# A two-layer decoder on one core: the inverse roots of six normalisation sites move from a bit-pattern seed with three Newton steps to a power on GpSimd with one

## The chip, the cores and the metric

The kernel runs on one core of a Trainium2 chip. The core has five engines, each with its own instruction queue that it works through in order: PE (TensorE, matrix products, with its weight loads shown as PEld), DVE (VectorE), ACT (ScalarE), POOL (GpSimd) and SP (SyncE, which here only issues DMAs). They wait for each other through semaphores. The metric is the time of one execution on the device in microseconds. The median of three executions of the kernel before is 1645.03 us (1643.46 to 1653.15).

## The reference

The inputs are x of 4 batches x 512 tokens x 512 features and a context of the same shape. Two layers of three blocks each follow, and after every block the sum with the block's input is normalised:

```
x = layernorm(x + L0_attention(x))            # stage A
x = layernorm(x + L0_cross_attention(x, ctx)) # stage B
x = layernorm(x + L0_ffn(x))                  # stage C, 8-bit activations, ternary weights
x = layernorm(x + L1_attention(x))            # stage D
x = layernorm(x + L1_cross_attention(x, ctx)) # stage E
x = layernorm(x + L1_ffn(x))                  # stage F, 4-bit weights

def layernorm(x): return (x - mean(x)) / sqrt(var(x) + 1e-5)   # over the 512 features
# at the end of L1_ffn: y / sqrt(mean(y * y) + 1e-6)
```

What the change touches is the inverse square root in these: one number per token, so 512 numbers per batch and normalisation. They lie in a tile of 128 partitions x 4.

## The kernel before

A task is one stage of one batch: A0 to A3, B0 to B3 and so on to F3, in that order. The function `lanes` runs up to two tasks at a time, step by step in turn: when a task reports "next", the following one is started beside it. So the last steps of B3, with its normalisation, lie beside the beginning of C0, those of C0 beside C1, and those of F0 beside F1. Further generators (`BESIDE`) load and prepare the weights of a later stage beside an earlier one. Within a task the class `Pipe` puts off an operation by so many steps. What this gives is the order of the program; a planner of the language then sets the order in each engine's queue from the dependences and its own estimates of the durations, and it may move an instruction past others, DMAs on SP too. Only the names below matter for the change.

**Roots.** `ln_rsqrt` (L185) adds 1e-5 to the four variances of a batch, giving `ve`, and then forms 1/sqrt(ve). For the pairs in `LOG_SEED` (all of A, B, D and E except B3 and E3) it takes a seed from ACT, exp(-0.5 ln ve), and one Newton step. For all others, which are B3, E3, C0 to C3 and F0 to F3, it calls `rsqrt`: two integer instructions on DVE (L162, L163) make a seed from the bit pattern, and three Newton steps follow. A Newton step is three DVE instructions (L170, L171, L172). Stage F calls `rsqrt` a second time, for the root of its own mean square (tile `fm`, after L1117). That is 14 calls of `rsqrt` in all: ten on an `ln` tile and four on an `fm` tile.

**Around the roots.** `ln_stats` (L176, L177) gathers mean and variance of a 128x512 tile. After the root `finish` normalises four such tiles (L200, DVE) and stores them (L203, SP); the next stage loads them again from DRAM (L217). In F the root of `fm` scales the four accumulators `facc` into x (L1121), which frees their four PSUM banks.

**Stage F.** For each of 11 chunks of the inner width, TensorE forms gate and up in four groups each (L1104, into PSUM tiles `fg`); ACT (L1062, L1065) and DVE (L1068) scale the groups and add them up, and so free the banks; POOL adds a part (L1072); ACT applies Silu (L1076), DVE multiplies (L1080), ACT and POOL split the product into a high and a low part (L1085, L1086), and TensorE adds the second product into `facc` (L1095). There are eight PSUM banks, four of which `facc` holds.

**Stage C.** TensorE forms `pg` and `pu` (L645, L647), DVE and ACT make the gated product (L616, L617, L621, L623), POOL its low part (L624), TensorE the Hadamard transform, which goes through DRAM (`had_scratch`, stored at L636, loaded again as `z`). In the second half DVE takes maxima (L659) and quantises (L680), and TensorE forms `dn` (L699), which DVE adds (L703).

Of the kernel before, what the change touches and what calls it, by code (L numbers as in the profile page):

```python
# [14 lines left out]
I32 = mybir.dt.int32  # L15
U8 = mybir.dt.uint8
AF = mybir.ActivationFunctionType
ALU = mybir.AluOpType
# [4 lines left out]
P = 128  # L23
NT = 4
MAGIC = 12582912.0
RSQRT_SEED = float(0x5F3759DF)
O_BUFS, T_BUFS, X_BUFS, W_BUFS = 69, 13, 12, 4


# [12 lines left out]
class Pipe:  # L42


    def __init__(self):
        self.todo = []
# [21 lines left out]
class Net:  # L68
    def __init__(self, ctx, tc, args):
        self.tc = tc  # L70
        self.nc = tc.nc
        self.a = args
        self.n = 0
        pool = lambda name, **kw: ctx.enter_context(tc.tile_pool(name=name, **kw))
        self.const = pool("const", bufs=1)
        self.op = pool("op", bufs=O_BUFS)
        self.tp = pool("tp", bufs=T_BUFS)
        self.xp = pool("xp", bufs=X_BUFS)
        self.wp_ = pool("wp", bufs=W_BUFS)
        self.small = pool("small", bufs=4)  # L80
        self.psum = pool("psum", bufs=8, space=PSUM)
        nc = self.nc
        tc.keep_in_program_order(nc.scalar.preload_act_table_set(LOG_EXP))
        self.ident = self.c("ident", [P, P])
        make_identity(nc, self.ident)
        self.ident16 = self.c("ident16", [P, P], BF16)
        nc.vector.tensor_copy(self.ident16, self.ident)
        self.ones = self.c("ones", [P, P])
        nc.gpsimd.memset(self.ones, 1.0)
        scratch = lambda name, shape: nc.dram_tensor(name, shape, F32, kind="Internal").ap()  # L90
        self.had_scratch = scratch("had_scratch", (2, 2048, 512))
        self.xd = [args["x"]] + [scratch(f"x{i}", (B, S, D)) for i in range(1, 6)] + [args["out"]]
        self.bg, self.table = {}, None
        self.gu, self.dn = {}, []
        self.pre = {}
        self.w1 = {}
        self.mean, self.scale = {}, {}
        self.tern = {name: {} for name in self.TERNARY}
# [58 lines left out]

    def rsqrt(self, ve, s):

        nc = self.nc  # L160
        sh, y, t = s[:, 0:4], s[:, 4:8], s[:, 8:12]
        nc.vector.tensor_scalar(sh.bitcast(I32), ve.bitcast(I32), 1, None, ALU.logical_shift_right)  # L162
        nc.vector.tensor_scalar(y.bitcast(I32), sh.bitcast(I32), -1.0, RSQRT_SEED, ALU.mult, ALU.add)  # L163
        for _ in range(3):
            self.newton(ve, y, t)
        return y

    def newton(self, ve, y, t):
# [1082 lines left out]
```

## Time and profile before

| | |
|---|---|
| median of three executions | 1645.03 us (1643.46 to 1653.15) |
| profiled execution, own time | 1649.59 us |
| its span | 1647.9 us |
| mean granted TensorE clock | 0.982 |
| DVE: the two integer instructions of a seed, x14 each | some 0.16 us each, undisturbed |
| DVE: one instruction of a Newton step, 128x4, median | 0.154 to 0.161 us |
| stage F from F0's first normalisation to the end | from about 1315 us |

The profile is one execution. Its page gives the busy time of each engine, groups of instructions by source line, and the chain of waits: from the last instruction back to what released it, step by step. The line numbers are those of the kernel before. A timeline row gives start, duration, engine, line, operation, output and inputs, and, in brackets, how long the engine had stood idle before and what released it. Releasers are inferred.

### The profile page before, as it was taken

What the parts mean: (1) busy time and instruction counts of PE and PEld (TensorE: products, weight loads), DVE (VectorE), ACT (ScalarE), POOL (GpSimd) and SP (SyncE); (2) the same over time, 40 slices, a digit from 0 to 9 for tenths busy, and PEclk for the clock granted to TensorE, in tenths of its full rate; (3) what the DMA queues carried; (4) which work ended last, traced back from release to release, by engine and by line L of the source; (5) the groups of instructions that cost most, each with busy time, mean ns of one, the idle gap of its engine ahead of it and who ended that gap; (6) DMA issues with size and microseconds to landing.
All of it is one profiled execution on the core that took longest, in us unless ns stands there. A gap on an engine that the chain in (4) does not pass through costs nothing.

```text
span 1647.9 us, 25494 instructions
## 1 busy us (share of the span) xinstructions
PE 1543.2 (94%) x8215; PEld 1106.6 (67%) x8246; DVE 1244.6 (76%) x2684; ACT 1011.3 (61%) x2177; POOL 666.1 (40%) x672
## 2 busy tenths in 40 slices
PE   7999999999999899899999999999998989999995
PEld 5888785444545664467777767777676766686874
DVE  6486589999875678967575666756879899979795
ACT  5333337988777777777696755968543444454542
POOL 6663654556435204420434342342333344333332
PEclk9999999999999999999999999999999999999998
DMA  6043344454125524861433323233445432011000
GB/s 244 29 147 122 122 162 138 133 171 159 52 95 176 186 82 138 245 176 62 130 76 78 78 81 109 69 79 76 154 153 178 142 102 61 24 54 51 1 26 25
DMA packets 103237, 180.76 MB, mean 110 GB/s; under 512 B 16561, under 2 KB 18609, under 8 KB 103105
## 3 DMA queue, kind: packets, MB, share of 16 engines
q1 hardware_dynamic: 98976, 170.69, 33.2%
q0 software_dynamic: 4128, 8.46, 2.1%
q8 instruction: 65, 1.06, 0.3%
q14 instruction: 68, 0.55, 0.1%
HBM read 111.98 MB, written 41.94 MB: 93 GB/s over the span
## 4 chain that ended last, share of the span: by engine, by line
PE 59%; DVE 17%; ACT 9%; DMA 6%; issue 5%; POOL 3%; SPq 1%; DVEq 0%; ACTq 0%; POOLq 0%
PE fg L1104 7%; PE facc L1095 6%; PE dT L881 3%; PE bo L458 2%; ACT de L871 2%; DVE bsm L434 2%; DVE x L200 2%; PE pu L647 2%; PE bT L213 2%; DMA z<-had_scratch 2%; PE pg L645 2%; PE dn L699 2%; PE do L901 2%; PE dq L150 2%; PE bs L486 2%
## 5 line engine op out<-in xcount | busy, mean ns | idle before, releaser
L1068 DVE SCALAR_TENSOR_TENSOR fg<-fg,gs,fg 128x512 f32<-128x512 f32 x220 | 162.3, 744 | 36.5 <-PE fg L1104 17.3
L867 DVE CUSTOM_DVE_ANT_0 de<-ds,negm,thr 128x128 f32<-128x128 f32 (+3 forms) x256 | 126.3, 545 | 34.3 <-PE ds L856 31.2
L1104 PE MATMUL fg<-fxh,gu 128*128 128x512 f32 x352 | 144.2, 410 | 7.6 <-DVE fg L1068 4.6
L871 ACT ACTIVATE de<-de,dm 128x128 f32<-128x128 f32 (+3 forms) x256 | 143.1, 563 | 12.4 <-DVE dm L867 11.9
L1104 PE MATMUL fg<-fxl,gu 128*128 128x512 f32 x352 | 139.1, 395 | 0.0
L442 POOL TENSOR_SCALAR be<-be,bsm 128x512 f32<-128x512 f32 x128 | 95.8, 760 | 104.5 <-DVE bsm L440 74.8
L624 POOL TENSOR_TENSOR hl<-g,hh 128x512 fp32r<-128x512 f32 x64 | 84.1, 1321 | 114.1 <-ACT hh L623 93.4
L1072 POOL TENSOR_TENSOR fg<-fg,fg 128x512 f32<-128x512 f32 x44 | 60.8, 1382 | 128.6 <-ACT fg L1065 89.4
L436 ACT ACTIVATE be<-bs,bsm 128x512 f32<-128x512 f32 x128 | 87.2, 688 | 31.9 <-DVE bsm L434 30.0
L798 POOL TENSOR_TENSOR dql<-dqf,dqh 128x512 fp32r<-128x512 f32 x32 | 41.2, 1289 | 155.1 <-ACT dqh L797 120.9
L881 PE MATMUL dT<-ident,de 128*128 128x128 f32 x640 | 90.3, 279 | 7.6 <-ACT de L871 5.8
L1104 PEld LDWEIGHTS fg<-fxh,gu 128*128 128x128 f32 x352 | 67.1, 191 | 38.1 <-DVE fg L1068 14.2
L881 PEld LDWEIGHTS dT<-ident,de 128*128 128x128 f32 x640 | 72.3, 142 | 26.1 <-ACT de L871 12.7
L1062 ACT ACTIVATE fg<-fg,gs 128x512 f32<-128x512 f32 x88 | 60.4, 686 | 39.9 <-PE fg L1104 39.5
L713 PE MATMUL had<-had,z 128*128 128x128 f32 x512 | 74.0, 289 | 10.5 <-DMA z<-had_scratch 10.2
L434 DVE TENSOR_REDUCE bsm<-bs 128x1 f32<-128x512 f32 x128 | 83.3, 671 | 0.0
L1095 PE MATMUL facc<-p4h,fhh 128*128 128x512 f32 x176 | 71.7, 408 | 8.9 <-DVE fg L1068 6.2
L713 PEld LDWEIGHTS had<-had,z 128*128 128x128 f32 x512 | 66.9, 198 | 18.7 <-DMA z<-had_scratch 7.7
L458 PE MATMUL bo<-bpT,cT 128*64 128x512 f32 x256 | 76.8, 618 | 2.9 <-DVE bpT L449 1.6
L213 PEld LDWEIGHTS bT<-ident,be 128*128 128x128 f32 x512 | 55.0, 141 | 34.1 <-issue 12.3
L213 PE MATMUL bT<-ident,be 128*128 128x128 f32 x512 | 73.2, 281 | 3.8 <-POOL be L442 2.1
L1065 ACT ACTIVATE fg<-fg,gs 128x512 f32<-128x512 f32 x44 | 30.3, 688 | 75.1 <-PE fg L1104 75.1
(332 smaller groups left out, 4676.2 us busy)
## 6 DMA issues: line engine op xcount, KB each, us to landing
x<-x SPq DMA_DIRECT2D x176, 256.0 KB, 3.1
had_scratch<-hw SPq DMA_DIRECT2D x64, 256.0 KB, 2.0
z<-had_scratch SPq DMA_DIRECT2D x64, 256.0 KB, 6.1
stk<-dqh SPq DMA_DIRECT2D x192, 64.0 KB, 2.0
tw<-in_wg_t SPq DMA_DIRECT2D x32, 256.0 KB, 3.7
tw<-in_wu_t SPq DMA_DIRECT2D x32, 256.0 KB, 3.7
tw<-in_wd_t SPq DMA_DIRECT2D x32, 256.0 KB, 2.9
p<-in_gu_p SPq DMA_DIRECT2D x22, 256.0 KB, 2.8
```

The source lines that it names most:

```text
L213: self.nc.tensor.transpose(pt[:, i * P : (i + 1) * P], srcs[i][:, j * P : (j + 1) * P], self.ident)
L434: nc.vector.tensor_reduce(sm[:, h : h + 1], ps, AX.X, ALU.max, negate=True)
L436: nc.scalar.activation(e, ps, AF.Exp, bias=sm[:, h : h + 1], accum_out=sm[:, 2 + h : 3 + h])
L442: nc.gpsimd.tensor_scalar(es[h][i], es[h][i], sm[:, 4 + h : 5 + h], 1.0, ALU.mult, ALU.mult)
L458: nc.tensor.matmul(po[0][h * 64 : h * 64 + 64, :], cT[j][:, c : c + 64], pTs[h], start=j == 0, stop=j == NT - 1)
L713: nc.tensor.matmul(ps[:, c * P : (c + 1) * P], z[g * 4 + c][:, i * P : (i + 1) * P], self.had16, start=True, stop=True)
L867: nc.vector.tensor_tensor_reduce(es[i], ps, self.negm[:, 384 - P * i :], -1.0, self.thr[:, i : i + 1], ALU.add, ALU.min, n4[:, i : i + 1])
L871: nc.scalar.activation(es[i], es[i], AF.Exp, bias=n4[:, i : i + 1], scale=-1.0, accum_out=den[:, hh * 4 + i : hh * 4 + i + 1])
L881: nc.tensor.transpose(pt[:, o + (i - j) * P : o + (i - j + 1) * P], es[i][:, j * P : (j + 1) * P], self.ident)
L1068: nc.vector.scalar_tensor_tensor(y[u], ps, s, y[u], ALU.mult, ALU.add)
L1095: nc.tensor.matmul(acc[t], h[l][:, c], self.dn[i][r], start=i == 0 and n == 0, stop=i == 10 and n == 2)
L1104: nc.tensor.matmul(ps, self.gu[i, u][:, g * P : (g + 1) * P], xT[g][n], start=n == 0, stop=n == 1)
```

## The change

`rsqrt` no longer makes a seed from bits. GpSimd raises `ve` to the power of -1/2 by a `tensor_tensor` with a constant tile of -0.5 (`mhalf`, 128x4, set once at the start), and one Newton step on DVE follows instead of three. The 14 calls stay where they are in the program; those that take their seed from ACT are not touched. Each call so has one POOL instruction and three DVE instructions instead of eleven DVE instructions; in all DVE has 112 instructions fewer and POOL 15 more (14 powers and the memset).

```diff
-RSQRT_SEED = float(0x5F3759DF)
...
+        self.mhalf = self.c("mhalf", [P, NT])
+        nc.gpsimd.memset(self.mhalf, -0.5)
...
     def rsqrt(self, ve, s):
 
-        nc = self.nc
-        sh, y, t = s[:, 0:4], s[:, 4:8], s[:, 8:12]
-        nc.vector.tensor_scalar(sh.bitcast(I32), ve.bitcast(I32), 1, None, ALU.logical_shift_right)
-        nc.vector.tensor_scalar(y.bitcast(I32), sh.bitcast(I32), -1.0, RSQRT_SEED, ALU.mult, ALU.add)
-        for _ in range(3):
-            self.newton(ve, y, t)
+        y, t = s[:, 4:8], s[:, 8:12]
+        self.nc.gpsimd.tensor_tensor(y, ve, self.mhalf, ALU.pow)
+        self.newton(ve, y, t)
         return y
```

`newton`, which both call, is unchanged: t = y*y; t = -0.5*t*ve; y = (t + 1.5)*y.

The planner orders the queues anew. On DVE the Newton step that waits for the power follows L185 or L1117 directly at the four `fm` roots, in B3 and in C3, and elsewhere after one other instruction; the four normalisations (L200) come earlier against the neighbours. On POOL the power stands between neighbours whose order is almost the same as before. On SP, in C1 and C2, the stores of x and their reloads come ahead of the first stores to `had_scratch` and of one weight load. In the changed kernel the lines behind `rsqrt` are numbered two lower (L170 becomes L168, L1117 becomes L1115).

## The prediction, on record before the changed kernel had run

> **What bounds the kernel.** I read the engine totals first, then the gaps of TensorE, then the chain of waits around the code that changes.
>
> ```profile
> PE 1543.2 (94%) x8215; PEld 1106.6 (67%) x8246; DVE 1244.6 (76%) x2684; ACT 1011.3 (61%) x2177; POOL 666.1 (40%) x672
> ```
>
> TensorE computes for 94% of the span, so removed DVE time counts only where TensorE stands still for DVE, or after its last matmul. The fourteen roots lie at: the end of B3 (469.7 us), C0 (597 to 604), C1 (624 to 635), C2, C3 (within 700 to 790), E3 (1315 to 1326), two for each of F0, F1, F2 (from 1406.6, 1485.2 and 1562), and two for F3 in the tail. Here is the chain of waits that ended last, cut to 1405 to 1412 (some pieces between are not shown), where F0 ends and F1 begins (columns: start us, us, who):
>
> ```profile
> 1406.70 0.09 DVE fm L1117
> ...
> 1406.81 0.18 DVE fm L162
> ...
> 1407.02 1.19 DVE fm L163
> ...
> 1408.23 1.20 DVE fm L170
> ...
> 1409.45 0.04 DVE fm L171
> ...
> 1409.53 0.76 DVE fg L1068
> ...
> 1410.33 1.59 PE facc L1095 x4
> ```
>
> The reader is to see that TensorE waits here for L1068, which empties a PSUM bank, and L1068 stands in DVE's queue behind the root. Two of its tiny 128x4 instructions take 1.19 and 1.20 us instead of some 0.16. The timeline says why:
>
> ```profile
> 1406.87 1.30 POOL L1072 TENSOR_TENSOR fg<-fg,fg 128x512 f32<-128x512 f32 x1 [3.16 <-DVE fm L1117]
> ...
> 1408.11 1.28 POOL L1086 TENSOR_TENSOR fhl<-fg,fhh 128x512 fp32r<-128x512 f32 x1
> ...
> 1410.33 0.50 PE L1095 MATMUL facc<-p4h,fhh 128*128 128x512 f32 x1 [1.92 <-DVE fg L1068]
> ```
>
> L163 and L170 begin just after POOL's two 1.3 us instructions and end with them, while L1068 (one operand in PSUM) runs at 0.75 beside POOL elsewhere. I call that a collision. TensorE loses 1.92 us, and in the next 4.1 us its granted clock is 0.58 (1.7 us more). The same pair of collisions and the same 1.92 us gap stand at 1488.87 and 1567.39.
>
> In the tail (timeline from 1628) TensorE and POOL are done and DVE works alone:
>
> ```profile
> 1631.27 0.17 DVE L162 TENSOR_SCALAR fm<-fm 128x4 int32<-128x4 int32 x1
> ...
> 1632.86 0.16 DVE L170 TENSOR_TENSOR fm<-fm 128x4 f32<-128x4 f32 x1
> ...
> 1633.45 1.41 DVE L1121 SCALAR_TENSOR_TENSOR x<-facc,fm,x 128x512 f32<-128x512 f32 x2
> ```
>
> Eleven dependent instructions take 2.18 us, start to start 0.198 each; the last Newton step alone takes 1633.45 - 1632.86 = 0.59. The second root, 1639.78 to 1641.96, is the same again.
>
> **The price of a pow (p).** No row of before shows pow. The nearest rows on POOL (source line, out, shape, then busy us and mean ns):
>
> ```profile
> L581 POOL TENSOR_SCALAR cm<-cm 128x4 f32<-128x4 f32 x4 | 1.0, 251 | 1.6 <-DVE bsm L440 0.9 <-DVE am L669 0.4 <-DVE cm L578 0.3
> ...
> L142 POOL TENSOR_TENSOR wkl<-wk,wkh 128x512 fp32r<-128x512 f32 x1 | 1.7, 1729 | 0.0
> ```
>
> From below 0.25 us: same shape, plain arithmetic. From above 1.73, the longest plain instruction of POOL, as if each of four elements cost as much as 128 plain ones. I take 0.5: the 128x4 row is nearest, doubled because a power is a series and not one operation. A handover DVE to POOL is 0.09 (L1117 ends 1406.78, L1072 starts 1406.87), back 0.03 (L923 ends 1166.33, the L924 that waits for it starts 1166.36), together 0.12.
>
> First-use cost: the first tensor_tensor on POOL took 1.27 us, no more than the later 1.3, so no row shows code being loaded. [...]
>
> **Part by part.**
>
> *Tail, two roots.* Each loses 2.18 and gets 0.59 + 0.12 + 0.5 = 1.21. POOL's last work ended at 1626, so nothing collides. Gain 2 x 0.97 = 1.9 us, wholly on the path.
>
> *F0/F1, F1/F2, F2/F3, first root (fm).* In the new order L1117 is followed at once by the Newton step, which waits for pow. Behind it in DVE's queue stands the same L1068 that TensorE wants. On POOL pow lands between an L1086 and L1072 and finds POOL idle (since 1403.7). L1072's operands are there at 1406.74, so it starts right behind pow. So: pow 1406.87 to 1407.37; L1072 to 1408.7, L170 (two SBUF operands) stuck behind it; L1086 to 1410.0, L171 stuck; L172; L1068 at 1410.2 instead of 1409.53. That is 0.65 us more wait, three times: loss 2.0. If only L170 is caught, L1068 comes at 1409.0 (gain 0.5); if none, at 1408.0 (gain 1.5). I take two, as POOL is first at both. Then L1121 and the statistics, formerly behind six L1068, come right after the first; the four facc banks that they free stand in for those that the later L1068 free.
>
> *F0 to F2, second root (ln), and E3.* Its steps lie between L1068s: a lone 128x4 instruction there costs under 0.1 us, since the neighbours overlap it. So the eight removed save mainly collisions (L185 1.26, L163 1.18, L171 0.71, L172 0.67 in F0: 3.2 us). But TensorE has no gap from 1411 to 1440, so at F I credit nothing. pow is covered: one L1068 (0.7) lies between L185 and the waiting L170, against 0.12 + 0.5; cover ends at p = 0.6. POOL is idle at 1419.4 to 1424.9, where pow falls. The 1.00 gap at 1440.57, behind four norms (L200), moves forward with them. In E3 two collisions (L170 0.81, L171 1.27) stand before TensorE gaps of 0.67 and 0.44: gain 0.7.
>
> *C0 to C3 and B3.* In B3 and C3 no instruction lies between L185 and the wait. B3: L616 comes 0.5 us later, and one L621 falls behind all four norms (about 1.3). TensorE has no gap over 0.3 from 460 to 490, with four pg/pu pairs of work ahead: nothing. C0, C2, C3: no gap beside them that is put down to DVE: nothing. C1: 2.7 us of collisions, and a gap of 1.07 at 638.75 for L616 behind the norms: gain 0.5.
>
> *Moved transfers.* On SP in C1/C2 the stores and reloads of x3 now stand ahead of the first had_scratch stores and a w1 load; in F0 three packed-weight loads swap neighbours. The z reloads wait for the last stores, which keep their places: 0, with 1.5 either way. One added 128x4 memset, 0.09 us while POOL idles to 5.36: nothing.
>
> Sum: -1.9 + 2.0 - 0.7 - 0.5 = -1.1 us. Against the profiled execution's own 1649.6 that gives 1648.5; that execution was 4.6 above the median of the runs (1645.0), to which I apply the same difference: **1644**. One percent (16 us) is about what a measurement can tell from no change.
>
> **Rivals.**
> 1. *Pow is slow* (ends slower). In DVE's queue everything behind the waiting L170 stops. At most 14 sites pay per us of p: 2 in the tail, 3 fm, 4 ln in E and F above 0.6, 5 in B and C above 0.6. Net loss starts near p = 0.65. At 1.73: tail +0.5, fm 3 x 1.9, ln 4 x 1.1, B and C half of 5 x 1.2, less 1.2: +13, or 1658. Over 1% from p near 2; 5 us would give 1645 + 14 x 4.4 = 1707. For: nothing bounds a power. Against: only 512 elements.
> 2. *The collisions vanish at the F boundaries* (faster). L1068 comes 1.5 earlier, the gap shrinks to 0.4 and the low clock with it: 3 x (1.5 + 1.7) + 1.9 + 1.2 = 12.7, or 1632. For: gaps of 1.0 (1440.57) and 1.5 (1329.31) are followed by clock 1.00. Against: L1072 stands ready behind pow.
> 3. *It does not do what it says*: interleaved steps were free anyhow, and a pow of 0.8 to 1.4 eats the tail's gain (gone at 2.18 - 0.59 - 0.12 = 1.47) while the fm waits grow: at 1.4, tail -0.1, fm +4.7, ln +3.2, B and C +2, less 1.2, or +8.6: 1646 to 1654.
>
> **Numbers.** Forecast (p 0.25 to 0.8, 1641 to 1648): 0.55. Rival 3, 1646 to 1654: 0.2. Rival 2, part or whole: 0.13, a tenth of it over 1%. Rival 1, p over 1.4: 0.12, nearly all over 1%. The range 1636 to 1655 leaves out rival 1 and the far half of rival 2, under 0.2 together. Faster by over 1%: 0.02; within: 0.87; slower: 0.11.
>
> **What will show it.** A POOL row of fourteen 128x4 tensor_tensor at L162 of the new numbering, mean near 500 ns, none far longer. In the tail: from L1115 (old L1117) to the first L1119 some 1.4 us instead of 2.4. At the F boundaries: L168 and L169 at 1.2 us each and TensorE's gap at 2.0 to 2.6; if it is under 1 with clock 1.00, rival 2. I am wrong if pow takes over 1 us, or if TensorE waits for DVE in C.

## The result: 0.46% slower

The changed kernel takes 1655.59 us (median of 15 executions, 1649.66 to 1660.52); the kernel before, beside it on the same chip, 1647.28 us (15 executions). The ratio is 1.0046, with a 95% interval of 1.0034 to 1.0058: 7.6 us slower where 1.1 us faster was forecast, and 0.6 us beyond the end of the range given. The profiled execution of the changed kernel took 1654.74 us, its span is 1653.0 us; before it was 1649.59 and 1647.9. The forecast of 1644 stood on a median of three executions of the kernel before, 1645.0; with 15 it is 1647.3, so 2.3 us of the distance between 1644 and 1655.6 are the base and not the change. The prediction took 16 us for the least that can be told from no change; with 15 executions of each kernel the interval is 2 us to either side.

The engine totals of the changed kernel, from its page:

```profile
PE 1544.1 (93%) x8215; PEld 1107.9 (67%) x8246; DVE 1225.0 (74%) x2572; ACT 1011.8 (61%) x2177; POOL 676.0 (41%) x687
```

DVE has 112 instructions and 19.6 us of busy time less, and the kernel is slower all the same. The groups of POOL, split by shape (busy us and mean ns of one, then idle time before):

```profile
L162 POOL TENSOR_TENSOR ln<-ln,mhalf 128x4 f32<-128x4 f32 x10 | 10.3, 1029 | 48.5 <-DVE ln L183 31.3 <-PE pu L645 17.1
L162 POOL TENSOR_TENSOR fm<-fm,mhalf 128x4 f32<-128x4 f32 x4 | 4.1, 1017 | 14.7 <-DVE fm L1115 14.7
```

A power of 128x4 takes 1.02 to 1.03 us on average, where 0.5 was taken. The first one of the execution (469.77, at the end of B3) took 1.04.

The chain of waits at the boundary of F0 and F1, restricted to that stretch (start us, us, who):

```profile
1410.32 1.03 POOL fm L162
...
1411.37 1.24 DVE fm L168
...
1412.64 1.21 DVE fm L169
...
1413.96 0.76 DVE fg L1066
...
1414.76 1.19 PE facc L1093 x4
```

The timeline of the same place (start us, us, engine, line, operation; in brackets the idle time before, and what ended it):

```profile
1410.32 1.02 POOL L162 TENSOR_TENSOR fm<-fm,mhalf 128x4 f32<-128x4 f32 x1 [3.15 <-DVE fm L1115]
...
1411.31 1.27 POOL L1070 TENSOR_TENSOR fg<-fg,fg 128x512 f32<-128x512 f32 x1
1411.37 1.23 DVE L168 TENSOR_TENSOR fm<-fm 128x4 f32<-128x4 f32 x1 [1.13 <-POOL fm L162]
...
1412.54 1.27 POOL L1084 TENSOR_TENSOR fhl<-fg,fhh 128x512 fp32r<-128x512 f32 x1
...
1414.76 0.50 PE L1093 MATMUL facc<-p4h,fhh 128*128 128x512 f32 x1 [2.88 <-DVE fg L1066]
```

DVE now stands 1.13 us for the power, then runs into both collisions that the prediction expected, and TensorE's gap has grown from 1.92 to 2.88 us. The tail, from the timeline:

```profile
1637.20 0.17 DVE L1115 TENSOR_SCALAR fm<-fm 128x4 f32<-128x4 f32 x1 [7.14 <-ACT fsq L1112]
1637.45 1.02 POOL L162 TENSOR_TENSOR fm<-fm,mhalf 128x4 f32<-128x4 f32 x1 [5.36 <-DVE fm L1115]
1638.50 0.16 DVE L168 TENSOR_TENSOR fm<-fm 128x4 f32<-128x4 f32 x1 [1.13 <-POOL fm L162]
...
1639.09 1.41 DVE L1119 SCALAR_TENSOR_TENSOR x<-facc,fm,x 128x512 f32<-128x512 f32 x2
```

From L1115 to L1119 it is 1.89 us, before 2.38: each of the two roots gains 0.5. Elsewhere only E3 is seen to gain.

**Where the time went.** To compare two traces I take the start of each TensorE instruction, counted from the first one, and subtract: the offset. Its places are counted from there too and so are 6 us lower than in the timelines. Between the changed kernel and before it is about 0 up to 520 us, +2.1 at 580, +5.4 at 610 and +6.0 from 770 to 1200; it falls to +3.4 before the first boundary of F, gains some 0.9 at each of the three boundaries, and the tail takes 1.0 back. In these two executions the largest part thus arises in stages B3 to C3, for which the prediction had put down next to nothing.

### The profile page after: what moved, and what is told of

Its sections match the earlier page's. It is cut to its first block, busy times and chain, and to the rows that moved or that the text cites. A ratio compares the mean times of both kernels' runs of the same rounds, so it can differ in the third digit from the quotient of the medians.

```text
span 1653.0 us, 25402 instructions
## 1 busy us (share of the span) xinstructions
PE 1544.1 (93%) x8215; PEld 1107.9 (67%) x8246; DVE 1225.0 (74%) x2572; ACT 1011.8 (61%) x2177; POOL 676.0 (41%) x687
## 4 chain that ended last, share of the span: by engine, by line
PE 54%; DVE 19%; ACT 11%; DMA 6%; issue 5%; POOL 3%; SPq 1%; POOLq 0%; DVEq 0%; ACTq 0%
PE fg L1102 6%; PE facc L1093 5%; DVE bsm L432 3%; PE dT L879 3%; ACT de L869 2%; PE pu L645 2%; DVE x L198 2%; PE pg L643 2%; PE do L899 2%; DVE fg L1066 2%; PE dn L697 2%; PE dq L151 2%; PE dq L152 2%; PE dq L153 2%; PE bo L456 1%
## 5 line engine op out<-in xcount | busy, mean ns | idle before, releaser
L869 ACT ACTIVATE de<-de,dm 128x128 f32<-128x128 f32 (+3 forms) x256 | 143.2, 563 | 12.4 <-DVE dm L865 11.9
L1070 POOL TENSOR_TENSOR fg<-fg,fg 128x512 f32<-128x512 f32 x44 | 58.9, 1340 | 126.3 <-ACT fg L1063 78.6
L796 POOL TENSOR_TENSOR dql<-dqf,dqh 128x512 fp32r<-128x512 f32 x32 | 41.3, 1291 | 153.5 <-ACT dqh L795 121.1
L211 PEld LDWEIGHTS bT<-ident,be 128*128 128x128 f32 x512 | 54.9, 141 | 34.2 <-issue 10.4
```

What stands on the lines that cost most here:

```text
L211: self.nc.tensor.transpose(pt[:, i * P : (i + 1) * P], srcs[i][:, j * P : (j + 1) * P], self.ident)
L869: nc.scalar.activation(es[i], es[i], AF.Exp, bias=n4[:, i : i + 1], scale=-1.0, accum_out=den[:, hh * 4 + i : hh * 4 + i + 1])
```

## Experiments

Two theories at first. **Price**: DVE stands still for a power that takes 1.03 us, and TensorE follows. **Order**: the planner, which takes a power for a cheap instruction, moved the four norms ahead of the scales that the quantising in C waits for, and that costs. A third, **Collision**, puts the loss at the boundaries of F. Later, **Wait** (only the time in which DVE has nothing else in its queue costs) stands against **Neighbour** (a running power slows what runs beside it). Ratios are to the kernel before on the same chip, "us" is the ratio's difference times 1647; "stood" is DVE's time in standing for GpSimd's result at the roots, by the trace's list of waits.

| kernel | ratio (95% interval) | us | stood, us |
|---|---|---|---|
| changed kernel | 1.0046 (1.0034 to 1.0058) | +7.6 | 14.7 |
| the same again (11) | 1.0045 (1.0030 to 1.0060) | +7.4 | |
| 1 cheap instruction instead | 0.9993 (0.9982 to 1.0004) | -1.2 | 4.3 |
| 2 two powers in a row | 1.0120 (1.0102 to 1.0139) | +19.8 | 28.4 |
| 3 power in B3 and C alone | 1.0038 (1.0024 to 1.0052) | +6.3 | 4.0 |
| 4 power in E3 and F alone | 1.0023 (1.0012 to 1.0034) | +3.8 | 10.7 |
| 5 covered in B3 to C2 | 1.0028 (1.0014 to 1.0042) | +4.6 | 11.8 |
| 6 covered there and at fm | 0.9996 (0.9983 to 1.0009) | -0.7 | 10.4 |
| 7 no power, two steps | 1.0011 (0.9997 to 1.0026) | +1.8 | 0 |
| 8 before, fm root later | 0.9997 (0.9983 to 1.0011) | -0.5 | 0 |
| 9 two powers, covered | 1.0075 (1.0053 to 1.0097) | +12.4 | 19.1 |
| 10 power in E3 and F, fm covered | 0.9986 (0.9973 to 0.9999) | -2.3 | 9.2 |
| 12 cheap instruction in B3 and C alone | 1.0010 (0.9994 to 1.0026) | +1.6 | 0.6 |

### 1 and 2: the price alone, in the same order

```diff
-        self.nc.gpsimd.tensor_tensor(y, ve, self.mhalf, ALU.pow)
+        nc.gpsimd.tensor_scalar(y, ve, 0.0, 0.0005 if site[0] == "f" else 0.5, ALU.mult, ALU.add)
```

> All 14 powers are replaced by a cheap GpSimd instruction of the same place, tile and operand: y = 0*ve + a constant (0.5 on the ln tiles, 0.0005 on the fm tiles). Left out is the power itself, so the seed and with it the output is not the reference's. The order of the instructions on every engine is that of the changed kernel. The nearest row, L581, has 0.25 us for such an instruction, so the wait at each root should fall from 1.13 to some 0.35 us. Theory ORDER (the planner's new order in stage C, where the four norms stand ahead of the scales that the quantising waits for, carries the loss, +6 us by the end of C): the offset of TensorE against before stays at about +5 to +6 us at 800 to 1000 us; only the tail (2 x 0.78) and the three F boundaries (3 x 0.78) gain: some 1655.6 - 3.9 = 1651.7 us, still 4 us above before. Theory PRICE (the 1.03 us of a power, on which DVE stands, carries the loss): the offset at 800 us falls by up to 5 x 0.78 = 3.9 us as well, to about +2, and the time to 1648 us, equal to before. Theory COLLISION (the boundaries of F are what costs): two collisions stay at each boundary, with TensorE's gaps there at about 1.9 us again, and the stage from 1400 to 1640 us gives back its +2.8.

```diff
+        nc.gpsimd.tensor_tensor(sh, ve, self.mhalf, ALU.pow)
         nc.gpsimd.tensor_tensor(y, ve, self.mhalf, ALU.pow)
```

> Each root has two powers in a row on GpSimd, the first into a spare part of the tile: the price of a root rises from 1.03 to some 2.06 us; the order of all other instructions is that of the changed kernel. Theory PRICE: every site pays, up to 14 x 1.03 = 14 us above the changed kernel, 1665 to 1670 us. Theory ORDER: in C most of the wait lies beside other work; the tail pays 2.06, the three fm boundaries 3 x 1.03, a part of the rest: some +5 to +8, 1661 to 1664 us. Theory COLLISION: the fm boundaries alone pay, with TensorE's gap there 1 us longer each, and the tail: +5, 1661 us.

Measured: 1645.29 and 1667.31 us; Price had the second, and the first lies below what any of the three theories gave. The three kernels differ in nothing but what GpSimd needs for a root: 0.19, 1.02 and 2.03 us, and by the ratios the time moves by 8.7 and 12.2 us. Order falls as the main cause: with the same order the cheap instruction is no slower than before, and its offset at 800 us is +0.25. Collision falls too, as the larger part is in C. Against the time that DVE stands, the slope is 0.84 and 0.89 us per us: on average over the 14 roots nearly every microsecond of standing is paid. Root by root it is not the same.

The rows of the Newton steps that wait, in the changed kernel (timeline of DVE at the end of B3, in C0, C1, C2 and C3):

```profile
470.85 0.16 DVE L168 TENSOR_TENSOR ln<-ln 128x4 f32<-128x4 f32 x1 [1.16 <-POOL ln L162]
...
600.87 0.16 DVE L168 TENSOR_TENSOR ln<-ln 128x4 f32<-128x4 f32 x1 [0.56 <-POOL ln L162]
...
631.02 0.16 DVE L168 TENSOR_TENSOR ln<-ln 128x4 f32<-128x4 f32 x1 [0.57 <-POOL ln L162]
...
767.04 0.16 DVE L168 TENSOR_TENSOR ln<-ln 128x4 f32<-128x4 f32 x1 [0.56 <-POOL ln L162]
...
795.98 0.16 DVE L168 TENSOR_TENSOR ln<-ln 128x4 f32<-128x4 f32 x1 [1.16 <-POOL ln L162]
```

With the cheap instruction only the first and the last are left (experiment 1, same view):

```profile
470.56 0.16 DVE L177 TENSOR_TENSOR ln<-ln 128x4 f32<-128x4 f32 x1 [0.32 <-POOL ln L166]
...
789.30 0.16 DVE L177 TENSOR_TENSOR ln<-ln 128x4 f32<-128x4 f32 x1 [0.32 <-POOL ln L166]
```

As the order is the same, the offset between the three can be followed step by step, and each step has its place:

| root | DVE stands: exp. 1, changed, exp. 2 | step, exp. 1 to changed | step, changed to exp. 2 |
|---|---|---|---|
| B3 (470) | 0.32, 1.16, 2.15 | +1.0 (between 525 and 550) | +1.0 |
| C0 (600) | 0, 0.56, 1.55 | +0.66, and +1.7 behind it | +1.0 |
| C1 (630) | 0, 0.57, 1.55 | +0.65 | +1.0 |
| C2 (767) | 0, 0.56, 1.55 | +0.65 | +0.2 and +0.65, and +1.7 behind it |
| C3 (796) | 0.32, 1.16, 2.15 | 0 | 0 |

At C0, C1 and C2 TensorE is later by about what DVE stood longer, at C3 by nothing. Experiments 3 and 12 below, which also differ in the price alone, repeat it with +0.65, +0.65 and +0.68 us at C0, C1 and C2 and nothing at C3. At B3 the second power costs 1.0 at once, at 471 us. That the first one's +1.0, 60 to 80 us behind the root, comes from there is not shown: experiments 3 and 12 have no such step. The pieces of 1.7 us are something else: a stretch of half clock. Stretches of one microsecond each behind TensorE's gap at 614.67 in the changed kernel (columns: busy time and count of PE, PEld, DVE, ACT, POOL, then the granted TensorE clock, DMA share, GB/s):

```profile
614.00:615.00 1.00, 0.33 (x2) 0.21 (x3) 0.95 (x3) 1.00 (x2) 0.00 (x0) 1.00 0.00 0
615.00:616.00 1.00, 1.00 (x4) 0.30 (x2) 0.00 (x0) 1.00 (x2) 0.00 (x0) 0.51 0.00 0
616.00:617.00 1.00, 1.00 (x4) 0.41 (x3) 0.64 (x2) 1.00 (x3) 0.00 (x0) 0.50 0.00 0
617.00:618.00 1.00, 1.00 (x4) 0.35 (x3) 1.00 (x5) 1.00 (x3) 0.00 (x0) 0.50 0.00 0
618.00:619.00 1.00, 1.00 (x5) 0.39 (x4) 0.67 (x3) 0.59 (x1) 0.00 (x0) 0.79 0.00 0
```

The gap before it was 1.94 us; in experiment 1 the same gap is 1.65 us, and the clock behind it stays at 1.00. The shortfall adds up to 1.70 us here: from 615.01 to 618.43, for 3.41 us, the clock is 0.50. One such stretch more, near 580 us, is the rest of the difference between experiment 1 and the changed kernel in this stage (their offset grows by 6.4 us from 440 to 800: 3.0 in steps, 3.4 in two stretches). That one is not tied to a root: experiments 4 and 8, whose B3 and C are those of the kernel before, have a stretch at 580.7 as well, and the kernel before has none. Nor does the stretch at 615 come every time: the changed kernel's second profiled execution (experiment 11) has the same gap of 1.94 us there, and the clock behind it stays at 1.00.

### 3, 4 and 12: which roots

```diff
+POW = "B3 C0 C1 C2 C3".split()              # experiment 4: "E3 F0 F1 F2 F3 fm0 fm1 fm2 fm3"
...
+        if site in POW:
             nc.gpsimd.tensor_tensor(y, ve, self.mhalf, ALU.pow)
             self.newton(ve, y, t)
+        else:                                # seed from bits and three steps, as before
```

> The power only at the five roots of B3 and C0 to C3; the other nine keep the bit seed and three Newton steps. In stages B and C the order is that of the changed kernel, from E3 on that of before. Theory ORDER: nearly the whole loss of C is here, and the gain in E3, F0 and the tail is not: +6 us, 1653 us, with an offset of +6 from 800 us to the end. Theory PRICE: at most 5 x 1.1 us, of which the eight removed instructions (5 x some 1.3 us) take back about all: 1647 to 1650 us. Theory COLLISION (loss at F): no difference to before, within 1.5 us.

> The power only at the nine roots of E3 and F (four ln and four fm of F, one of E3); B3 and C keep the bit seed and three Newton steps, and there the order is that of before. Theory ORDER: E3 and F0 -2.5, three boundaries +0.9 each, the tail -1.0: about -0.8 us, equal to before, 1646.5 us. Theory PRICE: nine roots of 14: up to +5, 1652 us. Theory COLLISION: +2.8 at the boundaries and the rest nothing but the tail: +2, 1649 us.

Measured: +6.3 and +3.8 us; together more than the whole change (7.6), within their intervals. By the middle values B3 and C carry the larger part with five roots of 14, though the two intervals overlap. Experiment 3 came out where Order had it and above what Price gave (1647 to 1650). Experiment 4 was expected by Order to be equal to before, and isn't: its three boundaries have TensorE gaps of 2.88, 2.87 and 2.87 us instead of 1.92, and the tail gives back 1.0. In experiment 3 the loss exceeds the 4.0 us of standing, so I asked whether the rest is the order after all:

```diff
 # experiment 3, with
-            nc.gpsimd.tensor_tensor(y, ve, self.mhalf, ALU.pow)
+            nc.gpsimd.tensor_scalar(y, ve, 0.0, 0.0005 if site[0] == "f" else 0.5, ALU.mult, ALU.add)
```

> The third experiment's kernel (GpSimd at the five roots of B3 and C0 to C3 alone), with the cheap instruction y = 0*ve + 0.5 in place of the power; the power is left out, so the output is not the reference's. The order on every engine is that of the third experiment, whose time was 1.0038 of before, +6 us, though DVE stood only 4.0 us for its powers. Theory WAIT: some 3 us of it go, 1.0020 or less. Theory ORDER: what the third experiment lost beyond the wait, 2 to 3 us, is the new order in C and stays: 1.0015 to 1.0025. If all of it was wait and the half-clock stretches that follow the gaps: 0.9995 to 1.0005.

Measured: 1.0010, that is +1.6 us (-1.0 to +4.3), 4.7 below experiment 3, with intervals that just overlap. So most of what stage C loses goes with the power's price, in the time as in the steps above. Whether the new order in C costs a further microsecond or two can't be told from this.

### 5 and 6: the same power, with work in front of the wait

```diff
-        self.newton(ve, y, t)                # in rsqrt
+        if later is None:
+            self.newton(ve, y, t)
+        else:
+            later(ve, y, t)
...
+    def behind(self, ve, y, t):
+        with self.tc.issue_after(self.last.ins):     # the latest L614, L619 or L1066
+            self.newton(ve, y, t)
...
+        self.ln_rsqrt(ln, phase, b, lambda *a: pipe.later(3, self.behind, *a))
...
+        todo = []
+        r = self.rsqrt(ve, fm[:, 8:20], lambda *a: todo.extend(a))
+        for _ in range(5):
+            yield
+        self.behind(*todo)
```

`issue_after` has the planner queue what stands in it behind the instruction named. The line of `ln_rsqrt` stands in `finish`, and with it experiment 5 is complete; the last five lines, the fm root in `l1_ffn`, come on top in experiment 6.

> All 14 powers stay on GpSimd at their full price of 1.03 us, but in B3, C0, C1 and C2 the Newton step that waits for the power is queued on DVE behind two to five other 128x512 instructions instead of none or one (C3, E3 and F keep the order of the changed kernel, and nearly all else does). Theory WAIT (DVE standing still for the power is what costs, since in C TensorE follows DVE's delay one to one): DVE waits for no power in B3 to C2, the offset of TensorE at 800 to 1000 us falls from +6.0 to about +0.3, where the cheap instruction had it, and the time from 1655.6 to some 1650 us. Theory NEIGHBOUR (the power running on GpSimd slows what runs beside it, whether or not DVE waits): the offset stays above +4, and the time at 1654 to 1656 us.

> As the run before, and at the three boundaries of F the Newton step of the fm root stands behind two L1066 (the one that TensorE waits for is the first of them), by issuing it five steps later. Theory WAIT: TensorE's gap of 2.87 us at each boundary falls under 1 us, which gives 3 x 2 = 6 us and one to three half-clock stretches of 1.7 us: 1650 - 8 = 1642 us, faster than before. Theory BANKS (the four accumulators are then freed some 3 us later, and TensorE stands there instead): no more than 1 us better than the run before, 1649 to 1651 us.

In experiment 5 DVE stands for no power in B3, C0, C1 and C2 (C3's 1.16 us is left, as at F); 2.8 us less standing, and the time is +4.6 us instead of +7.6: the 3 us that were uncovered, though the two intervals overlap. The offset at 800 us was expected at +0.3 and is +5.65: a miss. In that execution it stands at +1.95 already at 440 us, before the first root, and at +6.5 at 580, before that of C0; from 580 to 800, where C0 to C2 lie, it falls by 0.9, while that of the changed kernel grows by 3.9. Kernels that leave B3 and C untouched have +1.5, +2.6 and -1.2 at 800 us (experiments 4, 8 and 10), so an offset against before in this stage is uncertain by 2 us or so in a single execution; only between kernels of one order, where each step has its place, do I read it closely.

In experiment 6 the row that shows the boundary is this:

```profile
1412.69 0.50 PE L1109 MATMUL fg<-fxh,gu 128*128 128x512 f32 x1 [1.08 <-ACT fg L1067]
```

The gap has fallen from 2.87 to 1.08 us at each of the three boundaries, with no half clock behind it. A second gap of 1.17 to 1.55 us some 16 us later has come in its place, because DVE stands 2.15 us for the ln root there (1.50 in the changed kernel). So neither theory's number was right: 1647.1 us lies between 1642 and 1649.

### 7 and 8: without any power

```diff
-        for _ in range(3):
+        for _ in range(2):                   # kernel before, experiment 7
             self.newton(ve, y, t)
```

> No power at all: the kernel before with its bit seed, and two Newton steps instead of three at all 14 roots. Left out is one Newton step, so the roots are less exact. Theory WAIT (no handover to GpSimd, three instructions of some 0.2 us less per root): the tail gains 2 x 0.59 = 1.2, the three boundaries up to 0.6 each, C up to 2: 1642 to 1645 us. Theory ORDER (any change of the planner's order in C costs some us): 1648 us or more.

```diff
+        for _ in range(5):                   # kernel before, experiment 8, in l1_ffn
+            yield
+        with self.tc.issue_after(self.last.ins):
             r = self.rsqrt(ve, fm[:, 8:20])
```

> The kernel before, with no power and three Newton steps; only the fm root of F is issued five steps later and so stands behind two of the L1068 on DVE, for whose bank TensorE waits at the boundary. If the queue of DVE at the boundary is what TensorE's 1.92 us gap comes from: 3 x 1.5 us of gap and up to three half-clock stretches of 1.7 us: 1637 to 1642 us. If the accumulators become the wait instead (BANKS): within 1.5 us of before.

Experiment 7 takes 42 instructions off DVE and gains nothing (+1.8, -0.5 to +4.3); of its two expectations Order had the number. It fits what the prediction had said of the ln roots in F, that a 128x4 instruction between two 128x512 ones is as good as free; in the tail, where nothing lies beside them, its traced execution gains 1.1. Experiment 8 takes TensorE's 1.92 us gap down to 0.48 to 0.50 at each boundary, now put down to L1124, which frees the accumulators, but three more of 0.32 to 0.47 appear within 20 us, and the time doesn't move: Banks had the number. (In its traced execution the offset does fall by 4.0 us from 1400 to 1600; the 12 executions do not bear this out.)

### 9 and 10: the cover put to the test, and a better kernel

```diff
 # experiment 6, with
+        self.nc.gpsimd.tensor_tensor(s[:, 0:4], ve, self.mhalf, ALU.pow)
         self.nc.gpsimd.tensor_tensor(y, ve, self.mhalf, ALU.pow)
```

> The two powers in a row of the second experiment (2.03 us a root), with the Newton steps queued later as in the sixth (behind two to five other DVE instructions in B3 to C2, behind two L1066 at the fm roots). Theory WAIT: what a power costs is only the part of it in which DVE has nothing else in its queue. Of the 2 us, 1.3 to 2 are covered at seven of the 14 sites, so the second power adds little there: some 0.8 us at each of B3 to C2 and of the fm roots at most, and 2 in the tail: 1647 + 2 + up to 5 = 1649 to 1654 us, against 1667 for the same powers uncovered. Theory NEIGHBOUR (a power costs by running): +11.7 over the sixth experiment, as the second power cost the changed kernel: 1658 to 1660 us.

```diff
 # experiment 4, with, in l1_ffn
+        todo = []
+        r = self.rsqrt(ve, fm[:, 8:20], "fm" + str(b), todo)
+        for _ in range(5):
+            yield
+        with self.tc.issue_after(self.last.ins):
+            self.newton(*todo)
```

> The candidate for a faster kernel: powers in E3 and F alone, as in the fourth experiment, with the fm root's Newton step behind two L1066; B3 and C as in the kernel before, with three Newton steps. Theory WAIT: the fourth experiment's time of +3.8 us against before, less what the sixth took off the fifth (5 us): 1 to 2 us under before, within what can be told from no change. Theory ORDER (the loss of the fifth and sixth kernels sits in C's new order): 4 us under before.

Experiment 9 takes 1660.2 us, the time that Neighbour gave. The place decides against Neighbour nevertheless. Against experiment 6, whose order it shares, the offset goes from -1.0 at 440 us to -2.3 at 800, where the same doubling without cover had cost 6.2 us. Within this it steps up twice, by 0.97 us at 612 and by 0.97 at 776, the places behind C0 and C2 at which the steps between experiment 1, the changed kernel and experiment 2 lie, and these are the two roots at which DVE now stands for the second power, 0.95 us each. At B3 and C1, where it does not stand, there is no such step, nor at C3. (From 520 to 583 the offset falls by 4.1 us, in places that belong to no root; what does this is not shown.) The larger loss is in F and the tail (+3.9 to +4.9 at each boundary, +2 in the tail), where DVE has not enough to do. The ln root of F0 in experiment 9 (timeline):

```profile
1424.96 1.02 POOL L162 TENSOR_TENSOR ln<-ln,mhalf 128x4 f32<-128x4 f32 x1
1425.95 1.01 POOL L163 TENSOR_TENSOR ln<-ln,mhalf 128x4 f32<-128x4 f32 x1
...
1426.99 1.22 DVE L176 TENSOR_TENSOR ln<-ln 128x4 f32<-128x4 f32 x1 [3.14 <-POOL ln L163]
...
1428.92 0.80 PE L1110 MATMUL fg<-fxh,gu 128*128 128x512 f32 x1 [3.19 <-DVE fg L1074]
```

The expectation's mistake was to count cover at the fm roots and forget the ln roots behind them: there the power waits in GpSimd's queue behind another instruction, DVE stands 3.14 us, and TensorE 3.19.

Experiment 10, the power in E3 and F with the fm roots covered, has the lowest ratio of all: 0.9986 (0.9973 to 0.9999), 2.3 us under before, at the edge of what can be told from no change and too wide to choose between its two theories. Experiment 11 is the changed kernel itself, run beside these two:

> The changed kernel itself, beside the two above on the same chip: 1.0046 of the time of before again, within 0.0012.

It gave 1.0045.

## Why the prediction was wrong

**The step "I take 0.5".** The power takes 1.02 us, between the ends 0.25 and 1.73, and twice the value taken. With 1.02 the prediction's own sum becomes: tail -0.9, fm 3 x 1.17 = +3.5, ln 4 x 0.42 = +1.7, B and C half of 5 x 0.42 = +1.0, less 1.2, together +4.1. Of the 8.7 us between forecast (-1.1) and result (+7.6) this one term is 5.2. Rival 3 had just this price (0.8 to 1.4) and this mechanism; it was given 0.2. Both signs that the prediction named for being wrong have come: the power takes over 1 us, and in C TensorE waits for DVE. (Rival 1's terms at 1.73 add up to +12.4 and not +13. Among the collisions of the ln root in F that were to go, the prediction counts L185, which stays; nothing was credited there.)

**The step "C0, C2, C3: no gap beside them that is put down to DVE: nothing".** It failed at C0 and C2, and so did the gain at C1; it held for C3. At B3, put at nothing as well, the second power of experiment 2 was paid; for the first it is not shown. I had looked for TensorE gaps whose releaser is DVE. The gaps in C are put down to ACT or to a DMA (`dn` waits 1.4 us in all for L691, `had` 10.2 us for the load of z), and these wait in turn for DVE: in the chain of waits L659 at 608.04 stands ahead of the L691 at 609.86, and L659 at 727.63 ahead of the load at 727.78. What should have been read is the busy time of DVE from each root on in the kernel before (stretches; columns as above):

```profile
469.50:479.50 10.00, 10.00 (x47) 4.50 (x45) 9.50 (x24) 5.45 (x9) 2.64 (x3) 1.00 0.43 149
...
595.00:605.00 10.00, 9.95 (x83) 8.09 (x83) 10.00 (x36) 6.45 (x11) 0.54 (x2) 1.00 0.01 2
624.00:640.00 16.00, 14.83 (x67) 7.09 (x67) 15.98 (x33) 9.28 (x17) 6.86 (x5) 1.00 0.31 113
...
760.00:770.00 10.00, 9.90 (x78) 7.48 (x79) 9.86 (x36) 7.30 (x11) 0.28 (x1) 1.00 0.44 150
788.00:798.00 10.00, 10.00 (x46) 8.28 (x45) 6.77 (x20) 4.02 (x7) 3.68 (x6) 1.00 0.63 164
```

At C0, C1 and C2 DVE (third pair) is busy 10.00 of 10, 15.98 of 16 and 9.86 of 10 us; at C3 6.77 of 10. A wait put into a full queue delays all behind it, and experiments 1 and 2 show just that split: C0 to C2 paid about one to one, C3 nothing. B3, where the second power was paid, has 9.50 of 10 behind its root; ahead of it, from 460 to 470, DVE is busy for only 5.14, so it is the time behind the root that has to be read. The share of 76% over the whole span says nothing of this.

**The step "pow is covered by one L1068" for the ln roots in F.** The cover was there, but GpSimd was not idle. The timeline of F0 in the changed kernel:

```profile
1424.72 1.29 POOL L1084 TENSOR_TENSOR fhl<-fg,fhh 128x512 fp32r<-128x512 f32 x1 [1.34 <-ACT fhh L1083]
...
1425.97 1.02 POOL L162 TENSOR_TENSOR ln<-ln,mhalf 128x4 f32<-128x4 f32 x1
1427.02 0.16 DVE L168 TENSOR_TENSOR ln<-ln 128x4 f32<-128x4 f32 x1 [1.50 <-POOL ln L162]
...
1427.91 0.50 PE L1102 MATMUL fg<-fxh,gu 128*128 128x512 f32 x1 [1.08 <-DVE fg L1066]
```

L183 had ended at 1424.74; the power began only at 1425.97, behind L1084, and DVE stood 1.50 us, with a gap of 1.08 on TensorE. The idle time of POOL had been read from the kernel before, where this L1086 (now L1084) starts only at 1427.53, behind the root's first steps. At F1 and F2 DVE stands the same 1.50 us, but TensorE has no such gap there; why, the clock below tells.

**What held.** The tail: with p = 1.02 the prediction's terms (2.18 - 0.59 - 0.12 - p) give 0.45 per root, measured 0.49 and 0.50. The handover: 0.08 to GpSimd and 0.03 back, against 0.12. The boundaries: both Newton instructions collide, 1.23 and 1.20 us, at all three; with p = 1.02 the gap should have grown by 1.17 and grew by 0.95. No first-use cost: the first power took 1.04 us and DVE stood 1.16 for it, as for the later ones in C3. E3: the offset falls by 0.9 us from 1300 to 1400, where a gain of 0.7 was forecast. The moved transfers: experiment 1 has them all and is not slower than before.

**What the sum had no term for** is that a stretch of half clock on TensorE can follow a new gap, as one of 3.41 us followed the gap at 614.67. Rival 2 alone counted 1.7 us at each boundary of F, as something to be won back. In the runs of experiment 11 the mean granted clock is 0.9793 for the changed kernel (6 executions) and 0.9827 for before (17): (1 - clock) x time is 34.2 and 28.5 us, 5.7 more (standard error 1.4) where the time is 7.6 longer. How much of the loss is clock does not follow from that. In the two profiled executions of the result the shortfall is the same (30.2 and 30.7 us), and the changed kernel's span is 5.1 us longer all the same. And a stretch of half clock is not always paid, as the two profiled executions of the changed kernel show. At F0/F1 the second alone has one, at F1/F2 the first alone, and yet the offset between them is +1.36 us at 1400, +1.34 at 1450 and +1.34 at 1550: TensorE has a second gap of 1.08 or 1.11 us, behind the ln root, where the clock stayed up, and one of 0.37 or less where it was low (experiment 11, F1, where it stayed up):

```profile
1508.63 0.50 PE L1102 MATMUL fg<-fxh,gu 128*128 128x512 f32 x1 [1.11 <-DVE fg L1066]
```

At C0 the same two differ by the stretch at 615, and there it is paid: the offset steps by 1.7 us and stays.

What stays open: a loss of up to some 2 us in C that goes with the order and not with the price (experiments 3, 7 and 12 leave room for it, none shows it), and how much of the 7.6 us is clock.

## What to carry to other kernels

Before an instruction is handed to another engine, read how busy the waiting engine is in the 10 us behind the place, not over the span, and not by the releasers of TensorE's gaps alone: at the roots of C the standing was paid in full where that queue was full (10.00 and 9.86 us of 10 at C0 and C2, 15.98 of 16 at C1), and not where a third of it was free (6.77 of 10 at C3), and removed instructions that lay between large ones gave nothing that could be measured (experiment 7: +1.8 us, -0.5 to +4.3). Here each microsecond that DVE stood cost 0.87 us on average, and taking away 112 small instructions, with the new order, was worth some 5 us in all. The 5 us are an estimate, the line through experiments 1, 2 and the changed kernel carried to no standing; 3.2 of it is the tail by its own rows, 2 x (2.18 - 0.59). If the handover must be, queue other work between the question and the answer, on the waiting engine, and look at the queue of the engine that answers as well.

## What the runs showed of the hardware

**GpSimd's power** costs 1.01 to 1.04 us for 128x4 (L162 of the changed kernel, 14 instances), where a multiply and add of the same shape takes 0.19 (experiment 1, 14 instances) and a tensor_tensor of 128x512 some 1.3 (L796 and L1070 of the changed kernel: means of 1.29 and 1.34). Two in a row took 1.04 + 1.00 at B3 (experiment 2) and 1.02 + 1.01 at F0 (experiment 9): there is no saving in the second.

**TensorE's clock after a gap.** Where the clock drops between 40 us and the tail, the shortfall is 1.70 or 1.71 us, or twice that: in the traces of the kernel before and of the changed one each such stretch runs at 0.50 and lasts 3.41 us, or 6.83 (twice, in before). At the boundaries of F, whose gap is of much the same length each time a kernel has it, I counted in thirteen traces how often a stretch of half clock went with it: gaps of 1.9 to 2.1 us, 9 of 18; 2.86 to 2.88 us, 9 of 12; 3.2 to 3.8 us, 6 of 6; 1.0 to 1.2 us, 0 of 16. Identical gaps of 1.92 us had it three times of three in the kernel before and never in experiment 7.

There a gap of 1.9 to 2.1 us on TensorE was followed by 1.7 us of missing clock every second time (9 of 18); what decides when it comes is not shown. Whether these are paid too depends on what TensorE waits for next, as C0 (the offset steps by 1.7 us) and the boundaries of F (+1.36 and +1.34, no step) show.
